# Two-layer graph network on one core: the first layer's products on 64 partitions, its loads by three chunks

## The chip, the cores and the metric

The kernel runs on one core of a Trainium2 chip. The metric is the device time of one execution, in microseconds, as the median of several runs. Engines are named as in the profile: PE is TensorE (PEld its weight loads), DVE is VectorE, ACT is ScalarE, POOL is GpSimd, SP is SyncE. SP issues nearly all plain transfers, POOL the indirect ones.

## The reference

There are N = 12500 nodes with 128 features and E = 400000 edges, sorted by their destination `dst`. With `ln` for a layer norm without weights, and a sum per destination node:

```python
h   = relu(ln(x))
e   = relu(concat(h[src], h[dst], edge_attr) @ We1 + be1)    # 320 -> 32
m   = relu(e @ We2 + be2)                                    # 32 -> 128
n   = relu(concat(h[dst], m) @ Wn1 + bn1)                    # 256 -> 64
msg = relu(n @ Wn2 + bn2)                                    # 64 -> 128
x1  = x + h + segment_sum(msg, dst)

h1  = relu(ln(x1))
H   = einsum('ni,rio->rno', h1, W)                           # 8 relations
out = x1 + relu(segment_sum((H[etype, src] + b[etype]) * weight, dst))
```

`edge_attr` has 64 values an edge; `etype` is one of 8 relations; `weight` is one number an edge.

## The kernel before, in words

**Nodes first.** A stage over all nodes (pools `n0` and `n1`) writes tables to DRAM. `tab_a` has each node's 32 values `h @ We1[:128]`, for the source side. `tab_cb` has the destination side's 64 + 32 values, split into three bf16 parts in three rows. The centring of x runs mostly on POOL. `rel_d` holds, for each chunk of edges, `dst` less the chunk's least `dst`, and other small tables hold the starts of chunks and spans.

**First layer** (pool `e0`). The edges go by chunks of 1024 (`CE` = `CT` x 128 = 8 tiles of 128): 391 chunks. Three chunks (`SC`) make a span, 131 of them, which shares one window of 128 destination nodes and one accumulator. For a chunk the class `Edges` does this:

- `gather_a` (line 358): eight indirect transfers on POOL, one for each tile of 128 edges, fetch rows of `tab_a` into `gb`. This tile has 16 buffers.
- `load_rel` (379) and `load` (373, 375): SP loads `relb` (one chunk's `rel_d`, broadcast to 126 partitions, 252 KB), `eat` (the edge attributes, turned, 256 KB) and `win` (42 nodes x 3 rows of `tab_cb`, 23.6 KB). These tiles have 4, 5 and 8 buffers.
- `ends_T` (383): DVE compares `relb` with the node numbers; `ohT`, 126 x 1024 in bf16, is a one-hot matrix of destinations.
- `first` (395, 398): PE forms `pre`, 128 partitions x 256 columns. The edges of a chunk lie as four quarters of 256 columns on four groups of 32 partitions. Two products with `w_ea` (which has We1's edge rows twice, on its diagonal) and four with `win` and `ohT`.
- `first_src` (403, 405): DVE turns the gathered rows in blocks of 32 x 32 (`agT`) and adds them to `pre`, giving `z`. `first_end` (409): ACT makes `h1` from it.
- `second` (416, 422): PE makes two tiles `pm0` and `pm1`, 128 x 512, by four products of 256 columns. Each takes 64 partitions of `h1` and a `w_e2` whose other half is zero. ACT makes `em` from them.
- `third` (428, 431, 434), `fourth` (441), `fourth_sum` and `fourth_end` (449, 450, 455): the node network, from `u` and `h2` to `pq` and `nm`. `nm` holds each message as a rounded part and the rest.
- `ends` (460) makes the one-hot matrix `oh` of the span's window, and `fifth` (465) multiplies it with `nm` into the accumulator `acc`.

The loop over chunks writes one step of several chunks at a time; step i holds `load(i + 3)`, the gather and `first` of chunk i, `second` and `third` of i - 1, `fourth` and what follows of i - 2, and `fifth` of i - 3. `in_order` makes SP, DVE, ACT and PE keep that written order; POOL has only the gathers. On SP a step's order is: loads of chunk i + 3; when i is a multiple of 3 the previous span's `xt` (631); then the stores of a span that has ended (644 `agg0_d`, 510 `x1_d`, 511 `out`); the next span's `aw` (472); and one step of `prepare`.

`prepare` makes what the second layer needs (the order of edges in `hidx_sb`, `rel_t`, `ew_sb`) by way of DRAM, one step per chunk from the first chunk on. Its tiles `raw`, `tr` and `hidx` have two buffers each.

When a span has ended, `rows_h` adds its sums to x and h, stores the rows x1 (to `x1_d`, and to `out`), and makes the second layer's table `tab_h` of 8 x 128 values for each of the window's nodes (lines 485 to 527).

**Second layer** (pool `e1`). POOL gathers a row of `tab_h` for each edge (line 950, 3128 gathers); DVE weights and adds them, PE adds them by node, and `add_out` (785 to 797) adds the sum to x1 and stores `out`. It starts when the whole of `tab_h` is written. A branch, `again`, serves inputs that this layout does not fit; it does not run here.

Of the kernel before, what the change touches and what calls it, by code (L numbers as in the profile page):

```python
# [19 lines left out]
P = 128  # L20
# [29 lines left out]
def gnn_kernel(  # L50
# [82 lines left out]
    b_e1 = const.tile([P, 1], F32, name="b_e1")  # L133
# [125 lines left out]
    with tc.tile_pool(name="n1", bufs=2) as pool:  # L259
# [103 lines left out]
    class Edges:  # L363
# [5 lines left out]
            self.pool, self.psum, self.iota, self.node = pool, psum, iota, node  # L369

        def load(self, c, row):
            self.eat = self.pool.tile([P, 512], F32, name="eat", bufs=5)
            nc.sync.dma_start(self.eat, ea[ds(c, 1), :, :].rearrange("o k e -> (o k) e"))
            self.win = self.pool.tile([WR, 96], BF16, name="win", bufs=8)
            nc.sync.dma_start(self.win, tab_cb[ds(row, WR), :])

        def load_rel(self, c):
            self.relb = self.pool.tile([WR, CE], BF16, name="relb", bufs=4)
            nc.sync.dma_start(self.relb, rel_d[c:c + 1, :].to_broadcast([WR, CE]))

        def ends_T(self):
            self.ohT = self.pool.tile([WR, CE], BF16, name="ohT", bufs=4)
# [3 lines left out]
        def ends_T_of(self, c, node):  # L386
# [14 lines left out]
        def first_src(self, gb):  # L401
            agT = self.pool.tile([P, 256], F32, name="agT", bufs=2)
            nc.vector.transpose(agT, gb.rearrange("p t f -> p (t f)"))  # L403
            self.z = self.pool.tile([P, 256], F32, name="z", bufs=2)
            nc.vector.tensor_add(self.z, self.pre, agT)  # L405

        def first_end(self):
            self.h1 = self.pool.tile([P, 256], F32, name="h1", bufs=2)
            nc.scalar.activation(self.h1, self.z, AF.Relu, bias=b_e1)  # L409

        def second(self):
            pms = [self.psum.tile([P, 512], F32, name=f"pm{h}") for h in range(2)]
            for i in range(2):
                for h in range(2):
                    rows = slice(64 * h, 64 * h + 64)
                    nc.tensor.matmul(pms[h][:, 256 * i:256 * i + 256],  # L416
                                     w_e2[rows, 2 * h + i, :], self.h1[rows, :],
                                     start=True, stop=True)
            self.em = []
            for h in range(2):  # L420
                em = self.pool.tile([P, 512], F32, name=f"em{h}", bufs=2)
                nc.scalar.activation(em, pms[h], AF.Relu, bias=b_e2)  # L422
                self.em.append(em)

        def third(self):
            u = self.psum.tile([P, 512], F32, name="u")
            for h in range(2):
                nc.tensor.matmul(u[64 * h:64 * h + 64, :], self.win[:, 0:64],
                                 self.ohT[:, 512 * h:512 * h + 512], start=True, stop=False)
# [32 lines left out]

        def fifth(self, acc, start, stop):
            for i in range(CT):
                nc.tensor.matmul(acc, self.oh[:, i, :],  # L465
                                 self.nm[:, i, :, :].rearrange("p q d -> p (q d)"),
                                 start=(start and i == 0), stop=(stop and i == CT - 1))

    def window0(pool, row, n):
# [33 lines left out]
                                       op0=OP.max, op1=OP.add)  # L503
        return x0

    def rows_h(pool, psum, row, x0, aw, banks):
# [4 lines left out]
        nc.sync.dma_start(out[ds(row, P), :], x1)  # L511
# [15 lines left out]
        nc.sync.dma_start(tab_h[ds(row, P), :], ht)  # L527


    with tc.tile_pool(name="e0", bufs=2) as pool, \  # L530
# [6 lines left out]
        chunks, spans = {}, {}  # L537
        active = []

        def node_step():  # L540
# [3 lines left out]
        def load(c):  # L544
            e = Edges(pool, psum, iota_p, nid_p)
            row = nc.values_load(cidx[0:1, c:c + 1], engines=[ENG.SP], min_val=0,
                                 max_val=3 * (N - 1),
                                 skip_runtime_bounds_check_because="a chunk's least dst is a node")
            e.load_rel(c)
            e.load(c, nc.s_assert_within(  # L550
                row, 0, 3 * (NP - WB), skip_runtime_bounds_check_because="WB < NP - N"))
            chunks[c] = e

        def prepare():
# [5 lines left out]
            for g in range(0, NTP, QT):  # L560
                m = min(QT, NTP - g)
                cols = slice(g, g + m)
                for given, table in ((dst_t, dst_d), (et, hidx_d), (ew, ew_d)):
                    raw = pool.tile([P, QT], F32, name="raw")
                    nc.sync.dma_start(raw[:, :m] if given is ew else raw[:, :m].bitcast(I32),
                                      given[:, cols])
                    yield
                    if given is dst_t:
                        nc.vector.tensor_copy(raw[:, :m], raw[:, :m].bitcast(I32))
                    elif given is et:  # L570
                        nc.vector.scalar_tensor_tensor(raw[:, :m], src_sb[:, cols], float(R),
                                                       raw[:, :m].bitcast(I32),
                                                       op0=OP.mult, op1=OP.add)
                    tr = pool.tile([P, QT], F32, name="tr")
                    nc.vector.transpose(tr[:, :m], raw[:, :m])
                    rows = table[cols, :].rearrange("(q r) (a j) -> a r q j", r=32, j=32)
                    for a in range(4):
                        nc.sync.dma_start(
                            rows[a], tr[32 * a:32 * a + 32, :m].rearrange("r (q j) -> r q j", j=32))
                    yield  # L580
            odd = pool.tile([P, NSP // QS], F32, name="odd", bufs=1)
            for i, s in enumerate(range(0, NSP, QS)):
                cols = slice(s * ST, (s + QS) * ST)
                hidx = pool.tile([P, QS * ST], F32, name="hidx")
# [235 lines left out]
    def again():  # L820
# [7 lines left out]
        with tc.tile_pool(name="g1", bufs=2) as pool, \  # L828
# [34 lines left out]
            with tc.For_i(0, NP, P) as row:  # L863
                xt = pool.tile([P, D], F32, name="xt")
                nc.sync.dma_start(xt, x[ds(row, P), :])
                x0 = plus_normed(pool, xt, *deviation(pool, xt))
                for _ in rows_h(pool, psum, row, x0, window0(pool, row, P), ("u", "u", "u")):
                    pass

        with tc.tile_pool(name="g2", bufs=2) as pool, \  # L870
# [174 lines left out]
```

## Time and profile before

| what | us |
|---|---|
| median of 5 runs | 7956.49 |
| lowest and highest | 7954.86, 7959.75 |
| the profiled execution | 7958.23 |
| its span, first to last instruction | 7956.4 |

| engine | busy us | share of the span |
|---|---|---|
| PE | 3299.8 | 41% |
| DVE | 5089.0 | 64% |
| ACT | 1627.8 | 20% |
| POOL | 5951.6 | 75% |

The share is a mean over stages that have different limits: the node stage fills some 50 us, the first layer lasts to about 4000 us and the second takes the rest. A row of the profile for a group of instructions reads: line, engine, operation, output <- inputs, count | busy us in all, mean ns of one | idle time of the engine just ahead of them, and what ended it. "issue" is time in which an engine waited for nothing that the profile shows. In the timeline a row has its start, its duration, and what it is; SPq is an issue of a transfer by SP. An f32 product of PE shows as two instructions (two passes), a bf16 or rounded one as one. A table by stage has the stretch, its length, an engine's busy us and (x) instructions, the clock that TensorE was granted, the DMA engines' busy share, and GB/s.

### The profile page before, as it was taken

Reading aid. Unit: us, or ns where it says so; the run is one execution under the profiler, and the core shown is the slowest. Engines: PE = TensorE matmul, PEld = TensorE weight load, DVE = VectorE, ACT = ScalarE, POOL = GpSimd, SP = SyncE. Lnnn points to the kernel's source line nnn. Section 1 sums busy time; section 2 is a strip of 40 time slices with the busy share of each in tenths; the row PEclk is TensorE's granted clock in tenths of the full one; section 3 lists DMA queues with packets and bytes.
Section 4 is the critical chain, followed back from the end, with each engine's and each line's share of the span. In section 5 each row is a group of like instructions: output and inputs, shape, how many; then the busy total and the mean of one; then the engine's idle time right before and its main releaser. Section 6 shows DMA issues by size and latency. Waiting matters only on the chain.

```text
span 7956.4 us, 66587 instructions
## 1 busy us (share of the span) xinstructions
PE 3299.8 (41%) x16589; PEld 1960.3 (25%) x16590; DVE 5089.0 (64%) x8155; ACT 1627.8 (20%) x3217; POOL 5951.6 (75%) x6273
## 2 busy tenths in 40 slices
PE   4877777777777777777720000000000000000000
PEld 3444444444444444444410000000000000000000
DVE  7887766666766766667655555555555555555555
ACT  3443333333333333333300000000000000000000
POOL 6777777777777777777757777777777777777776
PEclk7999899999999999999955555555555555555555
DMA  6655544333333333343322222222222222222222
GB/s 193 150 115 104 103 121 106 96 94 102 93 97 101 91 100 98 92 101 95 90 60 61 62 62 61 62 62 61 62 61 62 62 61 62 62 61 62 62 61 58
DMA packets 766351, 670.08 MB, mean 84 GB/s; under 512 B 382920, under 2 KB 587980, under 8 KB 765502
## 3 DMA queue, kind: packets, MB, share of 16 engines
q1 hardware_dynamic: 563608, 408.65, 17.8%
q0 software_dynamic: 200192, 256.65, 15.5%
q8 instruction: 135, 2.21, 0.1%
q14 instruction: 260, 2.13, 0.1%
q10 hardware_dynamic: 2156, 0.45, 0.0%
HBM read 526.07 MB, written 139.10 MB: 84 GB/s over the span
## 4 chain that ended last, share of the span: by engine, by line
POOL 55%; issue 24%; DMA 12%; DVE 6%; PE 2%; ACT 1%; SPq 1%; POOLq 0%; DVEq 0%; ACTq 0%
POOL hg L950 32%; POOL gb L358 23%; DMA gb<-tab_a,src_sb 8%; DMA hg<-tab_h,hidx_sb 2%; DVE nm L455 1%; DVE ohT L383 1%; DVE oh L460 1%; DMA xt<-in_x 0%; DVE pq L449 0%; ACT nm L450 0%; PE pq L441 0%; DMA tab_cb<-cs 0%; DVE ht L526 0%; PE acc L465 0%; DVE z L405 0%
## 5 line engine op out<-in xcount | busy, mean ns | idle before, releaser
L950 POOL DMA_INDIRECT hg<-tab_h,hidx_sb x3128 | 2954.5, 945 | 998.1 <-issue 929.6
L358 POOL DMA_INDIRECT gb<-tab_a,src_sb x3032 | 2868.9, 946 | 925.5 <-issue 828.9
L957 DVE TENSOR_TENSOR v<-hg,io_p 128x1024 f32<-128x1024 f32 x782 | 960.1, 1228 | 1689.5 <-DMA hg<-tab_h,hidx_sb 1681.6
L924 PE MATMUL acc<-hm,oh 128*128 128x256 f32 x782 | 299.6, 484 | 3621.9 <-DVE oh L921 3588.8
L924 PEld LDWEIGHTS acc<-hm,oh 128*128 128x128 f32 x782 | 195.8, 311 | 3726.8 <-issue 3692.0
L961 DVE TENSOR_REDUCE sm<-v 128x128 f32<-128x1024 f32 x782 | 958.9, 1226 | 9.0
L964 ACT CAST hm<-sm 128x256 fp32r<-128x256 f32 x391 | 145.6, 373 | 3778.2 <-DVE sm L961 3778.2
L441 PE MATMUL pq<-w_n,h 128*128 128x256 f32 x3128 | 846.0, 419 | 0.0
L403 DVE STREAM_TRANSPOSE agT<-gb 128x256 f32<-128x256 f32 x391 | 173.5, 444 | 893.7 <-DMA gb<-tab_a,src_sb 891.8
L465 PE MATMUL acc<-nm,oh 128*128 128x256 f32 x3128 | 563.5, 330 | 389.5 <-DVE a L478 280.9
L441 PEld LDWEIGHTS pq<-w_n,h 128*128 128x128 f32 x3128 | 644.3, 216 | 88.3 <-issue 0.3
L465 PEld LDWEIGHTS acc<-nm,oh 128*128 128x128 f32 x3128 | 471.7, 221 | 556.2 <-issue 356.4
L450 ACT ACTIVATE nm<-pq 128x512 fp32r<-128x512 f32 x782 | 441.8, 597 | 625.7 <-DVE pq L449 623.1
L455 DVE SCALAR_TENSOR_TENSOR nm<-pq,nm 128x512 fp32r<-128x512 f32 x782 | 503.7, 686 | 70.2 <-ACT nm L450 25.6
L449 DVE TENSOR_TENSOR pq<-pq,b_n 128x512 f32<-128x512 f32 x782 | 505.1, 691 | 1.5 <-PE pq L441 1.5
L422 ACT ACTIVATE em<-pm,b_e 128x512 f32<-128x512 f32 x782 | 491.5, 681 | 58.8 <-PE pm L416 58.1
L434 ACT ACTIVATE h<-u,b_n 128x512 f32<-128x512 f32 x391 | 268.6, 687 | 1131.7 <-PE u L431 1131.6
L416 PE MATMUL pm<-h,w_e 64*128 64x256 f32 x3128 | 493.2, 438 | 1.8 <-ACT h L409 1.8
L383 DVE TENSOR_TENSOR ohT<-relb,io_p 126x1024 bf16<-126x1024 bf16 x391 | 473.2, 1210 | 15.6 <-DMA relb<-rel_d 15.6
L460 DVE TENSOR_TENSOR oh<-io_p,rel_s 128x1024 fp32r<-128x1024 f32 x391 | 475.8, 1217 | 0.0
L431 PE MATMUL u<-em,w_msg 128*64 128x512 f32 x1564 | 415.7, 600 | 6.7 <-ACT em L422 6.5
L525 PE MATMUL u<-w_f,hT 128*128 128x512 f32 x520 | 294.3, 648 | 209.6 <-ACT h L434 206.1
(117 smaller groups left out, 3225.9 us busy)
## 6 DMA issues: line engine op xcount, KB each, us to landing
eat<-in_ea SPq DMA_DIRECT2D x391, 256.0 KB
relb<-rel_d SPq DMA_DIRECT2D x391, 252.0 KB
tab_h<-ht SPq DMA_DIRECT2D x131, 512.0 KB
hg<-tab_h,hidx_sb POOLq DMA_INDIRECT x3128
gb<-tab_a,src_sb POOLq DMA_INDIRECT x3032
aw<-agg_d SPq DMA_DIRECT2D x262, 64.0 KB
agg_d<-a SPq DMA_DIRECT2D x261, 64.0 KB
agg_d<-zeros SPq DMA_DIRECT2D x48, 256.0 KB
```

The costliest lines, as they stand in the source:

```text
L358: nc.gpsimd.indirect_dma_start(out=gb[:, t, :], out_offset=None, in_=tab_a, in_offset=bass.IndirectOffsetOnAxis(ap=idx(t), axis=0))
L383: nc.vector.tensor_tensor(self.ohT, self.relb, self.node.to_broadcast([WR, CE]), op=OP.is_equal)
L416: nc.tensor.matmul(pms[h][:, 256 * i:256 * i + 256], w_e2[rows, 2 * h + i, :], self.h1[rows, :], start=True, stop=True)
L441: nc.tensor.matmul(pq[:, 2 * i:2 * i + 2, :], self.h2[:, P * (2 * k + i):P * (2 * k + i) + P], w_n2, start=True, stop=True)
L449: nc.vector.tensor_add(pq, pq, b_n2[:, None, :].to_broadcast([P, 4, D]))
L455: nc.vector.scalar_tensor_tensor(nm[:, :, 1, :], pq, 0.0, nm[:, :, 0, :], op0=OP.max, op1=OP.subtract)
L460: nc.vector.tensor_tensor(self.oh, self.iota[:, None, :].to_broadcast([P, CT, P]), rel[:, :, None].to_broadcast([P, CT, P]), op=OP.is_equal)
L465: nc.tensor.matmul(acc, self.oh[:, i, :], self.nm[:, i, :, :].rearrange("p q d -> p (q d)"), start=(start and i == 0), stop=(stop and i == ...
L924: nc.tensor.matmul(acc[:, 0:2 * D], oh[:, q, :], hm[:, q, :, :].rearrange("p r d -> p (r d)"), start=begin and q == 0, stop=stop and q == 1)
L950: nc.gpsimd.indirect_dma_start(out=hg[:, t - c * CT, :], out_offset=None, in_=tab_hr, in_offset=bass.IndirectOffsetOnAxis(ap=hidx_sb[:, t: ...
L957: nc.vector.tensor_tensor(v, hg, w_p[:, q, t:t + CT, None].to_broadcast([P, CT, D]), op=OP.mult)
L961: nc.vector.tensor_reduce(sm[:, q, :], v.rearrange("p t d -> p d t"), AX.X, OP.add)
```

## The change

- `pre`, `z` and `h1` become 64 partitions x 512 columns. `first` has one product with `w_ea` of 512 columns and two with `win` (32 partitions and 512 columns each, the columns of `ohT` taken as two runs of 256). `z` is made by two additions of 64 x 256. `second` has two products of 512 columns, each on 32 partitions of `h1`. `w_e2` is 64 x 128 without zeros, and `b_e1` has 64 rows; their memset and four loads on ACT's queue are gone.
- The order of edges in `u` changes with it; `third` takes the same halves of `ohT`, and `fifth` the tiles of `nm` in an order that fits.
- `eat` and `relb` are loaded for three chunks by one transfer each, at the span's first chunk, into 3 and 2 buffers of that size. `win` is loaded for each chunk as before. `eat` now comes ahead of `relb`.
- `rows_h` does not store x1 to `out` in this path.
- `raw`, `tr` and `hidx` have one buffer each.

```diff
-    w_e2 = const.tile([P, 4, D], F32, name="w_e2")
+    w_e2 = const.tile([64, D], F32, name="w_e2")
...
-        nc.vector.memset(w_e2, 0.0)
...
-        for i in range(4):
-            nc.scalar.dma_start(w_e2[32 * i:32 * i + 32, i, :], we2)
+        for i in range(2):
+            nc.scalar.dma_start(w_e2[32 * i:32 * i + 32, :], we2)
             nc.scalar.dma_start(b_e1[32 * i:32 * i + 32, :], be1)
...
+        def half_T(self, h):
+            return self.ohT.rearrange("w (b a e) -> w a b e", b=2, a=2)[:, h, :, :]
+
         def first(self):
-            self.pre = self.psum.tile([P, 256], F32, name="pre")
-            for i in range(2):
-                nc.tensor.matmul(self.pre[64 * i:64 * i + 64, :], w_ea,
-                                 self.eat[:, 256 * i:256 * i + 256], start=True, stop=False)
-            for a in range(4):
-                nc.tensor.matmul(self.pre[32 * a:32 * a + 32, :], self.win[:, 64:96],
-                                 self.ohT[:, 256 * a:256 * a + 256], start=False, stop=True)
+            self.pre = self.psum.tile([64, 512], F32, name="pre")
+            nc.tensor.matmul(self.pre, w_ea, self.eat, start=True, stop=False)
+            for h in range(2):
+                nc.tensor.matmul(self.pre[32 * h:32 * h + 32, :], self.win[:, 64:96],
+                                 self.half_T(h), start=False, stop=True)
...
-            self.z = self.pool.tile([P, 256], F32, name="z", bufs=2)
-            nc.vector.tensor_add(self.z, self.pre, agT)
+            self.z = self.pool.tile([64, 512], F32, name="z", bufs=2)
+            for i in range(2):
+                cols = slice(256 * i, 256 * i + 256)
+                nc.vector.tensor_add(self.z[:, cols], self.pre[:, cols], agT[64 * i:64 * i + 64, :])
...
-            pms = [self.psum.tile([P, 512], F32, name=f"pm{h}") for h in range(2)]
-            for i in range(2):
-                for h in range(2):
-                    rows = slice(64 * h, 64 * h + 64)
-                    nc.tensor.matmul(pms[h][:, 256 * i:256 * i + 256],
-                                     w_e2[rows, 2 * h + i, :], self.h1[rows, :],
-                                     start=True, stop=True)
+            pms = []
+            for h in range(2):
+                pm = self.psum.tile([P, 512], F32, name=f"pm{h}")
+                rows = slice(32 * h, 32 * h + 32)
+                nc.tensor.matmul(pm, w_e2[rows, :], self.h1[rows, :], start=True, stop=True)
+                pms.append(pm)
...
+                at = i % 2 * 4 + i // 2 % 2 * 2 + i // 4
                 nc.tensor.matmul(acc, self.oh[:, i, :],
-                                 self.nm[:, i, :, :].rearrange("p q d -> p (q d)"),
+                                 self.nm[:, at, :, :].rearrange("p q d -> p (q d)"),
...
-        nc.sync.dma_start(out[ds(row, P), :], x1)
+        if to_out:
+            nc.sync.dma_start(out[ds(row, P), :], x1)
...
-            e.load_rel(c)
-            e.load(c, nc.s_assert_within(
+            s, k = divmod(c, SC)
+            if k == 0:
+                eat = pool.tile([P, SC, 512], F32, name="eats", bufs=3)
+                nc.sync.dma_start(eat, ea[c:c + SC, :, :].rearrange("c k e -> k c e"))
+                relb = pool.tile([WR, SC, CE], BF16, name="relb", bufs=2)
+                nc.sync.dma_start(relb, rel_d[c:c + SC, :].rearrange("(o c) e -> o c e", o=1)
+                                  .to_broadcast([WR, SC, CE]))
+                loaded[s] = eat, relb
+            eat, relb = loaded[s]
+            e.eat, e.relb = eat[:, k, :], relb[:, k, :]
+            e.load_win(nc.s_assert_within(
...
-                    raw = pool.tile([P, QT], F32, name="raw")
+                    raw = pool.tile([P, QT], F32, name="raw", bufs=1)
```

More of the change, by code (lines that the diff above doesn't have):

```diff
@@ L129, in gnn_kernel @@
     w_ea = const.tile([P, 64], F32, name="w_ea")
-    w_e2 = const.tile([P, 4, D], F32, name="w_e2")
+    w_e2 = const.tile([64, D], F32, name="w_e2")
     w_msg = const.tile([P, 64], F32, name="w_msg")
     w_n2 = const.tile([P, 2 * D], F32, name="w_n2")
-    b_e1 = const.tile([P, 1], F32, name="b_e1")
+    b_e1 = const.tile([64, 1], F32, name="b_e1")
     b_e2 = const.tile([P, 1], F32, name="b_e2")
@@ L371, in load, with load_win @@
         def load(self, c, row):
-            self.eat = self.pool.tile([P, 512], F32, name="eat", bufs=5)
+            self.eat = self.pool.tile([P, 512], F32, name="eat", bufs=2)
             nc.sync.dma_start(self.eat, ea[ds(c, 1), :, :].rearrange("o k e -> (o k) e"))
+            self.load_win(row)
+        def load_win(self, row):
             self.win = self.pool.tile([WR, 96], BF16, name="win", bufs=8)
             nc.sync.dma_start(self.win, tab_cb[ds(row, WR), :])
-        def load_rel(self, c):
-            self.relb = self.pool.tile([WR, CE], BF16, name="relb", bufs=4)
-            nc.sync.dma_start(self.relb, rel_d[c:c + 1, :].to_broadcast([WR, CE]))
         def ends_T(self):
@@ L403, in first_src @@
             nc.vector.transpose(agT, gb.rearrange("p t f -> p (t f)"))
-            self.z = self.pool.tile([P, 256], F32, name="z", bufs=2)
-            nc.vector.tensor_add(self.z, self.pre, agT)
+            self.z = self.pool.tile([64, 512], F32, name="z", bufs=2)
+            for i in range(2):
+                cols = slice(256 * i, 256 * i + 256)
+                nc.vector.tensor_add(self.z[:, cols], self.pre[:, cols], agT[64 * i:64 * i + 64, :])
         def first_end(self):
-            self.h1 = self.pool.tile([P, 256], F32, name="h1", bufs=2)
+            self.h1 = self.pool.tile([64, 512], F32, name="h1", bufs=2)
             nc.scalar.activation(self.h1, self.z, AF.Relu, bias=b_e1)
         def second(self):
-            pms = [self.psum.tile([P, 512], F32, name=f"pm{h}") for h in range(2)]
-            for i in range(2):
-                for h in range(2):
-                    rows = slice(64 * h, 64 * h + 64)
-                    nc.tensor.matmul(pms[h][:, 256 * i:256 * i + 256],
-                                     w_e2[rows, 2 * h + i, :], self.h1[rows, :],
-                                     start=True, stop=True)
+            pms = []
[4 more added lines that the diff above has]
+                pms.append(pm)
             self.em = []
@@ L428, in third @@
                 nc.tensor.matmul(u[64 * h:64 * h + 64, :], self.win[:, 0:64],
-                                 self.ohT[:, 512 * h:512 * h + 512], start=True, stop=False)
+                                 self.half_T(h), start=True, stop=False)
             for h in range(2):
@@ L504, in plus_normed, with rows_h @@
         return x0
-    def rows_h(pool, psum, row, x0, aw, banks):
+    def rows_h(pool, psum, row, x0, aw, banks, to_out=False):
         x1 = pool.tile([P, D], F32, name="x1", bufs=2)
@@ L536, in gnn_kernel @@
         nc.vector.tensor_copy(nid_p, nid)
-        chunks, spans = {}, {}
+        chunks, spans, loaded = {}, {}, {}
         active = []
@@ L573, in prepare @@
                                                        op0=OP.mult, op1=OP.add)
-                    tr = pool.tile([P, QT], F32, name="tr")
+                    tr = pool.tile([P, QT], F32, name="tr", bufs=1)
                     nc.vector.transpose(tr[:, :m], raw[:, :m])
@@ L583, in prepare @@
                 cols = slice(s * ST, (s + QS) * ST)
-                hidx = pool.tile([P, QS * ST], F32, name="hidx")
+                hidx = pool.tile([P, QS * ST], F32, name="hidx", bufs=1)
                 for table, to in ((dst_d, rel_t[:, cols]), (hidx_d, hidx), (ew_d, ew_sb[:, cols])):
@@ L866, in again @@
                 x0 = plus_normed(pool, xt, *deviation(pool, xt))
-                for _ in rows_h(pool, psum, row, x0, window0(pool, row, P), ("u", "u", "u")):
+                for _ in rows_h(pool, psum, row, x0, window0(pool, row, P), ("u", "u", "u"),
+                                to_out=True):
                     pass
```

## The prediction

> **What bounds the kernel now.** I read the page's busy shares and its chain first, then GpSimd's busy time by stage, then who waits for whom in the middle of the first layer, and last, in order of time, the stretch between the layers.
>
> ```profile
> PE 3299.8 (41%) x16589; PEld 1960.3 (25%) x16590; DVE 5089.0 (64%) x8155; ACT 1627.8 (20%) x3217; POOL 5951.6 (75%) x6273
> POOL 55%; issue 24%; DMA 12%; DVE 6%; PE 2%; ACT 1%; SPq 1%; POOLq 0%; DVEq 0%; ACTq 0%
> L950 POOL DMA_INDIRECT hg<-tab_h,hidx_sb x3128 | 2954.5, 945 | 998.1 <-issue 929.6
> L358 POOL DMA_INDIRECT gb<-tab_a,src_sb x3032 | 2868.9, 946 | 925.5 <-issue 828.9
> ```
>
> No compute engine is full; the chain is GpSimd's gathers and the "issue" between them. One gather takes 0.945 us and is followed by 0.30 us of issue: 1.25 us, eight to a chunk of 1024 edges, 10.0 us a chunk. Next, GpSimd's busy time and count of gathers, then granted clock, DMA share and GB/s; the last line lies in the second layer:
>
> ```profile
> 2000.00:2050.00 50.00, 37.79 (x40) 0.93 0.44 113
> ...
> 2004.00:2006.00 2.00, 1.70 (x2) 1.00 0.95 335
> 2016.00:2018.00 2.00, 1.39 (x3) 1.00 0.07 10
> ...
> 4150.00:4250.00 100.00, 75.62 (x81) 0.50 0.23 61
> ```
>
> Forty gathers in 50 us, whether the DMA engines are 95% or 7% busy and whatever clock TensorE has. Only the number of gathers and the time outside them make the total. From the gathers' own rows: the first starts at 53.62, the first layer's last ends at 3984.76, the second layer's run from 4030.08 to 7937.39, and the span ends at 7956.4. So 53.6 before, 3931.1 in the first layer (3128 at 1.25 would be 3910; 21 are lost at the start), 45.3 between the layers, 3907.3 in the second, 19.0 behind. The change can move only what it does to 53.6, 21 and 45.3, unless it makes the first layer's arithmetic slower than 10 us a chunk. The waits between 2000 and 3000 (100 chunks) say how far that is:
>
> ```profile
> DVE agT L403 <- DMA gb<-tab_a,src_sb: 270.0, 100, 5.0
> SPq L527 <- DVE a L477: 690.1, 34, 20.6
> ```
>
> VectorE waits 2.70 us of each chunk for the gather, 8.1 us in a span of three; SyncE is parked 20 us in each 30. That is the cover under which every first-layer edit lies. Busy time per chunk there: PE 7.56, DVE 6.96, ACT 3.68 us.
>
> **Part by part.**
>
> *First and second product.* Per chunk, from the groups between 2000 and 3000: `pre<-eat` 0.69 us (four passes of 256 columns, two column halves side by side), `pre<-ohT` 0.30, `pm<-h` 1.26 (eight passes, two row halves). After: one product of 512 columns in two passes on one column half. The row for passes one after another is `pq<-w_n,h`, 220.1 us for 800 of 256 columns, 0.275 each: 2 x 0.55 = 1.10, that is +0.41. Two `ohT` products of 512 columns: like L428, 41.8 us per 100 chunks, 0.42: +0.12. The second product is four passes of 512 in two row groups; its nearest row is `u<-em,w_msg`, four such passes in two column halves, 1.03: -0.23. PE: +0.30, 7.9 of 10 us, though eight of its matmul instructions a chunk are gone. The Trainium skill speaks against this part: in "TensorEngine Tiling (Array Packing)", "Performance Considerations", a stationary operand of at most 64 columns should be column-tiled, up to twice as fast. By that rule dropping the two halves would double the first product, +0.69 where I take +0.41, and PE would stand at 8.1. Row and rule then leave the total alone.
>
> *z and h1.* One 128x256 addition of 425 ns becomes two of 64x256. Time goes with columns, since the 128-column addition `a<-aw,acc` took 276; back-to-back additions overlap a little (two of 691 in 1.28). Bounds: +0.15 (256 columns at the 128-column price) to +0.95 (each like a 128x512 addition, 691); I take +0.40, the same columns twice: DVE 7.4 of 10. h1 goes from 501 ns to that of a 512-column activation, 681 to 687: +0.18 on ACT. All of it lies under the 2.70 us; without that cover +0.40 x 391 = 156 us. The stall stays where it is: the gather is still last.
>
> *Loads.* 782 loads of `relb` and `eat` become 262 of 756 and 768 KB; with `out` gone SyncE issues five transfers fewer a span, 0.35 us each, while parked: nothing. Bytes stay, less 131 x 64 KB. The skill's "DMA: Bandwidth & Descriptors", "Rules for kernel authors", says to coalesce many small transfers; "Anatomy of one DMA" gives a fixed 2.0 us for one (there for transfers issued from GpSimd), so 520 fewer would be an estimated 1040 us if they stood in line. Here they don't: GpSimd never waits for them. What the bundle moves is order on SyncE's queue. `xt` (L631), issued behind one chunk's 532 KB, is now behind 1548 KB; window 0 and the stores behind it likewise.
>
> ```profile
> 2008.10 0.34 SPq L631 DMA_DIRECT2D xt<-in_x  x1
> ...
> 2013.29 0.28 DVE L485 BATCH_NORM_STATS2 st<-xt 128x6 f32<-128x128 f32 x1
> ```
>
> VectorE reads it 5.2 us after its issue, without a wait. The extra 1016 KB at the 214 to 263 GB/s of 2008 to 2014 take 4.0 to 4.9 us. So VectorE waits 0 to 4.9 us a span at L485, and behind it in VectorE's order stand the next chunk's agT, z and ohT. With 3 x 0.40 for z at most 6.1 of the 8.1 us are used; I take 2, since nothing waits now. Waits for `relb` itself come later: its next group is issued some two chunks, 20 us, ahead of its first reader.
>
> *The start.* `relb` for chunk 0 lands behind 768 KB more, and group 1 is 1.5 MB instead of 0.5: the first chunks come up to 10 us later. Chunk 0's transpose starts at 134.4 now, 69.5 us behind its last gather, and the lag is down to 1.6 at chunk 47; from chunk 6 to 40 the steps average 8.8 us. With +0.4 for z and 0 to 1.6 (4.9 over three) for `xt`, 9.2 to 10.8. At the worst the lag grows from 80 by 0.8 a chunk until the preparing steps end (about chunk 90), to 147 us; `gb` has 16 buffers, 160 us of gathers, so GpSimd still never stops. From then a step is 7.3 (10 less 2.70) + 0.4 + 1.6 = 9.3 at most, and 300 chunks clear 210 us. `raw`, `tr` and `hidx` in one buffer: the next load of `raw` comes a step behind the store that already waited for `tr`, and the 38016 packets of 128 bytes to the tables took 13 ns each, 2.6 us of all 16 engines for a table, within the 15 us until `tr` is written again. Nothing. Ahead of the first gather the memset of `w_e2` (0.48 us) ended before the first `xg` landed: nothing; four ACT issues go and one `hT` moves ahead of the `sd` for which ACT stood still for 5.5 us at 28: 0 to -1.2, I take -0.5 (one quad's products). The 21 us lost early lie where VectorE's long operations run (gathers 4.8 and 4.5 us apart at 66 and 71, beside L286's 4.44); these are untouched: 0, with 3 either way.
>
> *Between the layers.* The path leaves the gather:
>
> ```profile
> 3984.66 0.33 SPq L511 DMA_DIRECT2D out<-x  x1
> 3985.63 1.33 SPq L631 DMA_DIRECT2D xt<-in_x  x2
> ...
> 3991.74 0.29 DVE L485 BATCH_NORM_STATS2 st<-xt 128x6 f32<-128x128 f32 x1 [7.57 <-DMA xt<-in_x]
> ```
>
> Without `out` the `xt` load is issued 0.65 us earlier (the spacing of L510 and L511), and no group is in front of it, since the last group went out before. Against it two z steps on VectorE's path, 2 x 0.40 = 0.80 (chunks 389 and 390), and h1 0.18. Sum +0.3; from -2 to +4.
>
> Sum: -0.5 + 0 + 0.3 = -0.2 on a span of 7956.4. The profiled execution took 7958.23, 1.8 over its span and 1.7 over the median of 7956.49. Prediction 7956.3 for the median.
>
> **The rivals.**
>
> *Slower: the bulk load in front of `xt`.* If VectorE waits at L485 so long that wait and z together pass 8.1 us in a span, the first layer becomes VectorE's, and each us beyond costs 131 us. It decides when `xt` comes 6.9 us later than now. For it: between 200 and 500 VectorE already waited 24.9 us in ten times for `xt`, and the load in the tail took 6.08 us behind the 512 KB of a `tab_h` store. Against: the bytes give at most 4.9. With 1 us too much 8087; a third of a us, 8000. Chance 0.06.
>
> *Slower: TensorE.* It stands at 7.9 us and decides at 10.0; at 10.2 a chunk, 0.2 x 391 = 78 us, it gives 8034. Chance 0.02.
>
> *Faster: the seams shrink.* The 45.3 us or the 21 would have to lose 16 in all; the profile shows 0.65 and 1.2 that can go. With a third out of the 45.3: 7941. Chance 0.03.
>
> *The change does not do what it says:* column halves lost, TensorE no lighter. Of the forecast's chance 0.7 is for this, 0.19 for halves kept some other way; it is in the sum: 7956.3 all the same.
>
> **How the numbers follow.** Forecast 0.89. In it -1.2 to 0 (start), 3 either way (early gathers), -2 to +4 (between), and 2 for the spread of five runs (7954.9 to 7959.8): added up, 7948 to 7966. A little toward the slow rivals' edge gives 7948 to 7968. A measurement of this kernel can tell 0.2%, 16 us, from no change: faster 0.03, within 0.89, slower 0.08.
>
> **What would show it.** Right: 40 gathers in every 50 us of the first layer; `agT`'s wait for `gb` down from 2.70 to about 1.6 us a chunk (2.3 if nothing waits for `xt`); `pre<-eat` near 1.1 us a chunk, z near 0.85; a new wait `st<-xt` of under 5 us a span; gap between the layers 43 to 49. Wrong: `agT`'s wait for `gb` gone, GpSimd waiting for `agT`, gathers apart by more than 1.25 us, or a first gather far from 53.

## The result, and the profile after

| | median us | lowest and highest | runs |
|---|---|---|---|
| before | 7957.05 | 7953.34, 7959.75 | 44 |
| changed | 7960.5 | 7957.2, 7963.4 | 24 |

The ratio is 1.0004, with a 95% interval from 0.9999 to 1.001: no difference that this measurement can tell from none. The profiled execution of the changed kernel took 7954.62 us, its span 7952.9.

The runs below fell on several chips: four on one where the kernel before takes 7951 us (an ordinary chip, in what follows, as is that of the table above), and eight on three others where it takes 10100 to 10211 (the slow chips). Their times are compared only with those of the kernel before on the same chip.

The page first: the engines' busy times, and the two groups of gathers.

```profile
PE 3526.3 (44%) x13461; PEld 1740.6 (22%) x13462; DVE 5297.2 (67%) x8545; ACT 1691.5 (21%) x3217; POOL 5943.6 (75%) x6273
L963 POOL DMA_INDIRECT hg<-tab_h,hidx_sb x3128 | 2951.5, 944 | 999.7 <-issue 941.1
L357 POOL DMA_INDIRECT gb<-tab_a,src_sb x3032 | 2864.2, 945 | 927.9 <-issue 798.8
```

TensorE has 3128 matmul instructions fewer and is busy for 226.5 us more; VectorE for 208 us more. POOL's gathers stand as they did: 0.945 us and 0.30 of issue. Then POOL by stage (busy us and count of instructions, granted clock, DMA share, GB/s):

```profile
2000.00:2050.00 50.00, 37.73 (x40) 1.00 0.40 111
4150.00:4250.00 100.00, 75.49 (x81) 0.50 0.23 60
```

Forty gathers in 50 us again. From the gathers' rows the parts of the span are 53.7 us ahead of the first, 3928.6 in the first layer, 46.7 between the layers, 3904.5 in the second, 19.4 behind the last (before: 53.6, 3931.1, 45.3, 3907.3, 19.0). Both layers are 2.6 to 2.8 us shorter here, the untouched one too: the period of the gathers differs by under 0.1% from one execution to another. So the shorter span of this one execution says nothing of the change.

What did change lies under that cover. VectorE's waits in the changed kernel, first from 200 to 1200 us, then from 3000 to 3900 (90 chunks); a row has the total, the times and the longest:

```profile
DVE st L487 <- DMA xt<-in_x: 156.5, 32, 10.2
DVE agT L402 <- DMA gb<-tab_a,src_sb: 5.5, 26, 0.5
```

```profile
DVE agT L402 <- DMA gb<-tab_a,src_sb: 121.4, 77, 3.9
DVE st L487 <- DMA xt<-in_x: 37.4, 22, 4.3
```

In the kernel before, from 200 to 1200:

```profile
DVE agT L403 <- DMA gb<-tab_a,src_sb: 141.3, 68, 5.9
DVE st L485 <- DMA xt<-in_x: 40.8, 18, 7.2
```

Early, VectorE now hardly waits for gathers, since it is behind them; it waits 4.9 us at each span for `xt`. The timeline of one such span:

```profile
608.01 0.40 SPq L555 DMA_DIRECT2D eats<-in_ea  x1
608.45 0.51 SPq L557 DMA_DIRECT2D relb<-rel_d  x1
...
610.25 0.37 SPq L643 DMA_DIRECT2D xt<-in_x  x1
...
618.80 0.29 DVE L487 BATCH_NORM_STATS2 st<-xt 128x6 f32<-128x128 f32 x1 [4.50 <-DMA xt<-in_x]
```

The 64 KB of `xt` go out behind 1.5 MB and are read 8.55 us after their issue; in the kernel before it was 5.2 us, without a wait, in the span shown ahead of the result (at 2008). How far VectorE falls behind is seen from each chunk's transpose `agT`: its start less the end of the chunk's last gather, worked out from the two rows.

| chunk | 0 | 6 | 30 | 50 | 90 | 120 | 150 | 200 | 300 |
|---|---|---|---|---|---|---|---|---|---|
| before, us | 69.5 | 50.3 | 21.3 | 1.6 | 2.3 | 3.6 | 1.9 | 1.5 | 2.1 |
| changed, us | 72.8 | 58.9 | 71.7 | 78.9 | 108.0 | 103.2 | 77.2 | 34.2 | 2.1 |

The lag that the kernel before worked off by chunk 47 grows until chunk 97, to 111.2 us, and is gone only by about chunk 230. POOL never stopped for it: `gb` has 16 buffers, 160 us of gathers, and at the closest POOL came to within 40 us of needing a tile that was still unread.

Two groups of TensorE and one of VectorE, from 2000 to 3000 (104 chunks; the first number behind the bar is busy us, the second the mean ns of one instruction):

```profile
L395 PE MATMUL pre<-eats,w_ea 128*64 128x512 f32 x207 | 119.2, 659 | 0.0
L417 PE MATMUL pm<-h,w_e 32*128 32x512 f32 x416 | 127.6, 692 | 0.0
L406 DVE TENSOR_TENSOR z<-pre,agT 64x256 f32<-64x256 f32 x208 | 86.6, 416 | 12.3 <-PE pre L397 0.2
```

That is 1.15, 1.23 and 0.83 us a chunk.

### The profile page after: what moved, and what is told of

It is laid out like the page before. It is cut to its first block, busy times and chain, and to the rows that moved or that the text cites. A ratio compares the mean times of both kernels' runs of the same rounds, so it can differ in the third digit from the quotient of the medians.

```text
span 7952.9 us, 59273 instructions
## 1 busy us (share of the span) xinstructions
PE 3526.3 (44%) x13461; PEld 1740.6 (22%) x13462; DVE 5297.2 (67%) x8545; ACT 1691.5 (21%) x3217; POOL 5943.6 (75%) x6273
## 5 line engine op out<-in xcount | busy, mean ns | idle before, releaser
L441 PE MATMUL pq<-w_n,h 128*128 128x256 f32 x3128 | 801.3, 402 | 0.0
L441 PEld LDWEIGHTS pq<-w_n,h 128*128 128x128 f32 x3128 | 611.0, 205 | 78.5 <-issue 0.8
L467 PE MATMUL acc<-nm,oh 128*128 128x256 f32 x3128 | 515.4, 310 | 88.5 <-DVE a L480 73.2
L467 PEld LDWEIGHTS acc<-nm,oh 128*128 128x128 f32 x3128 | 428.7, 203 | 420.8 <-issue 203.2
L395 PE MATMUL pre<-eats,w_ea 128*64 128x512 f32 x782 | 460.8, 674 | 92.3 <-DMA eats<-in_ea 91.3
L381 DVE TENSOR_TENSOR ohT<-relb,io_p 126x1024 bf16<-126x1024 bf16 x391 | 477.7, 1222 | 29.4 <-DMA relb<-rel_d 17.4
L431 PE MATMUL u<-em,w_msg 128*64 128x512 f32 x1564 | 488.7, 636 | 17.0 <-ACT em L422 16.5
L417 PE MATMUL pm<-h,w_e 32*128 32x512 f32 x1564 | 473.9, 684 | 1.9 <-ACT h L410 1.9
L528 PE MATMUL u<-w_f,hT 128*128 128x512 f32 x520 | 317.1, 694 | 206.5 <-ACT h L434 203.7
```

Of the source, the lines that this page charges most:

```text
L381: nc.vector.tensor_tensor(self.ohT, self.relb, self.node.to_broadcast([WR, CE]), op=OP.is_equal)
L441: nc.tensor.matmul(pq[:, 2 * i:2 * i + 2, :], self.h2[:, P * (2 * k + i):P * (2 * k + i) + P], w_n2, start=True, stop=True)
L467: nc.tensor.matmul(acc, self.oh[:, i, :], self.nm[:, at, :, :].rearrange("p q d -> p (q d)"), start=(start and i == 0), stop=(stop and i = ...
```

## The experiments

The theory: POOL's gathers, 1.25 us each, set the time; the layout and the loads only use up cover, the layout through VectorE and the loads through the wait for `xt`; 16 `gb` buffers are what keeps the early lag from POOL. The rivals: the lag has another cause than `xt`; the buffers are not what hides it; VectorE is the bound.

### Half the buffers, in both kernels

In `e1_after_gb8` (the changed kernel) and `e2_before_gb8` (the kernel before):

```diff
-        gb = gpool.tile([P, CT, 32], F32, name="gb", bufs=16)
+        gb = gpool.tile([P, CT, 32], F32, name="gb", bufs=8)
```

> The changed kernel with 8 buffers for gb instead of 16. Theory (GpSimd's gathers set the time and the 16 buffers hide how slow the first layer's arithmetic has become at the start): in the changed kernel's profile the gather of chunk i+8 starts up to 41 us before chunk i has been read, so GpSimd must stop for that long in all between chunks 20 and 110: 7960 + 41 = about 8000, and the gathers' own 1.25 us is seen everywhere else. Rival (the arithmetic has 8.1 us a span to spare all along, buffers don't matter): 7960.

> The kernel before with 8 buffers for gb. Theory: in its profile the gather of chunk i+8 never starts less than 15.6 us after chunk i was read, so nothing stops: 7957, within 3. Rival (half the buffers cost something by themselves, by contention or by the release of a buffer): the same loss as in the changed kernel, about 8000.

Measured on one chip, where the kernel before took 7951.22: the changed kernel 7979.89 us, ratio 1.0036 (1.0022 to 1.0051); the kernel before 7950.74, ratio 0.9999 (0.999 to 1.0009). The profiled executions took 8001.22 and 7964.42, and their first layers 3970.7 and 3933.0 us. The waits of POOL from 100 to 2000 us in `e1_after_gb8` show where:

```profile
POOL gb L357 <- DVE agT L402: 43.4, 25, 4.7
```

In the kernel before with 8 buffers that row is 0.3 us, once. Its lag is nearly that with 16 (16.7 us at chunk 35, with 16 it was 14.1), while the changed kernel's is held between 58 and 82 from chunk 6 to chunk 100: POOL has taken over the waiting. So the lag is real, and the buffers are what hides it. The size was 37 us by the profiled executions and 29 by the medians, where about 41 had been expected.

### `xt` ahead of the bulk loads

`e3_xt_first_gb8` is `e1_after_gb8` with one step moved:

```diff
-            if i + AHEAD < NC:
-                load(i + AHEAD)
             if i % SC == 0 and i:
                 spans[i // SC - 1] = Span(i // SC - 1)
+            if i + AHEAD < NC:
+                load(i + AHEAD)
```

> The changed kernel with 8 buffers for gb, and the span's xt issued ahead of the three-chunk loads instead of behind them. Theory (the lag comes from xt waiting behind 1.5 MB): VectorE's wait for xt between 200 and 1200 falls from 156 us to about 40 as before the change, the step there from 10.6 to about 9.4 us a chunk, the lag shrinks from the start, and the time is 7957 to 7965 although there are 8 buffers. Rival (the lag comes from the longer z, h1 and first product, or the DMA engines are simply busy with the bulk whatever the order): about 8000, as with 8 buffers alone.

Measured: 7953.73 us, ratio 1.0003 (0.9993 to 1.0012). VectorE's waits from 200 to 1200, first in `e1_after_gb8`, then here:

```profile
DVE st L487 <- DMA xt<-in_x: 157.8, 32, 11.2
```

```profile
DVE agT L402 <- DMA gb<-tab_a,src_sb: 93.8, 33, 7.4
...
DVE st L487 <- DMA xt<-in_x: 2.7, 1, 2.7
```

The wait for `xt` is gone, VectorE waits for gathers again, and the lag falls from 55.0 us at chunk 6 to 3.4 at chunk 50, with the new layout in place. What made the lag grow was the place of one 64 KB load in SyncE's queue.

### The layout without the coalesced loads

`e5_layout_alone` has the products, `z`, `h1` and the order of edges of the changed kernel; the loads of `eat` and `relb`, the store to `out` and the buffers of `raw`, `tr` and `hidx` are those of the kernel before. Against the changed kernel:

```diff
-            s, k = divmod(c, SC)
-            if k == 0:
...
-            e.eat, e.relb = eat[:, k, :], relb[:, k, :]
-            e.load_win(nc.s_assert_within(
+            e.relb = pool.tile([WR, CE], BF16, name="relb", bufs=4)
+            nc.sync.dma_start(e.relb, rel_d[c:c + 1, :].to_broadcast([WR, CE]))
+            e.load(c, nc.s_assert_within(
```

> The 64-partition layout alone: eat and relb loaded for one chunk at a time as before the change, x1 still stored to out, 16 buffers for gb. Theory (xt behind the bulk load makes the lag): the lag starts near 70 us as in both and falls by some 0.7 us a chunk (a step of 8.8 + 0.4 = 9.3 between chunks 6 and 40), gone by chunk 110; wait for xt between 200 and 1200 near 41 us; time 7957 to 7961. Rival (the layout makes it): the lag rises to about 100 us at chunk 90.

Measured in one run: 7953.31 us, beside 7951.22 for the kernel before. VectorE's waits from 200 to 1200:

```profile
DVE st L487 <- DMA xt<-in_x: 51.8, 25, 4.6
DVE agT L402 <- DMA gb<-tab_a,src_sb: 40.7, 31, 6.1
```

The lag falls from 53.9 us (chunk 6) to 25.5 (45) and 1.5 (80). From chunk 6 to 40 a chunk takes 9.35 us where the kernel before takes 8.81; of these 0.54 us `z` is 0.41. With `e3_xt_first_gb8` this parts the two bundles: the layout slows the catching up, the loads turn it round.

### On the slow chips: the loads alone, `z` twice, the order at the seam

Four kernels met chips where the kernel before took 10210 us and, for `e7r_z_twice` and `e6br_tail_before`, 10100; `e7_z_twice` and `e6b_tail_before` come three times under three names. `e4_loads_alone` is the kernel before with the loads by three chunks and the single buffers of `raw`, `tr` and `hidx`; it still stores to `out`. `e7_z_twice` writes each addition of `z` of the changed kernel twice:

```diff
-                nc.vector.tensor_add(self.z[:, cols], self.pre[:, cols], agT[64 * i:64 * i + 64, :])
+                for _ in range(2):
+                    nc.vector.tensor_add(self.z[:, cols], self.pre[:, cols],
+                                         agT[64 * i:64 * i + 64, :])
```

`e6_tail` (the changed kernel) and `e6b_tail_before` (the kernel before) rewrite only the order at the end of the first layer:

```diff
+            if i == L - 2:
+                for s in range((L - 1) // SC, NS):
+                    spans[s] = Span(s)
             next(prepared, None)
...
         for s in range((L - 1) // SC, NS):
-            if s not in spans:
-                spans[s] = Span(s)
-                spans[s].deviate()
+            spans[s].deviate()
...
         valued(L - 2)
+        chunks[L].first_src(gb)
+        chunks[L].first_end()
         node_step()
         ended(L - 2)
+        chunks[L].second()
...
-        chunks[L].first_src(gb)
-        chunks[L].first_end()
         node_step()
-        chunks[L].second()
```

> The three-chunk loads alone, on the layout of before (128 partitions by 256 columns), x1 still stored to out, 16 buffers for gb. Theory (xt behind the bulk load makes the lag, the layout adds 0.4 to 0.7 us a chunk): wait for xt between 200 and 1200 about 150 us as in the changed kernel, the lag neither falls nor rises much up to chunk 90 (10.6 less 0.5 = 10.1 us a chunk), 60 to 80 us there, and then falls faster than in the changed kernel; time 7951 to 7957. Rival (only both together make it): the lag falls as before the change, gone by chunk 50.

> The changed kernel with each of the two z additions done twice (the same values again), 0.85 us more of VectorE a chunk. Theory (what counts is the pace while behind, 10.6 us a chunk up to chunk 90 and 9.1 from 120 on in the changed kernel, and not the 1.35 us a chunk that VectorE still waits late in the layer): 11.4 and then 10.0 us a chunk, so the lag reaches the 150 us of 16 buffers near chunk 70, GpSimd is stopped for some 45 us in all, and about 150 us of lag are left at the end: the gap between the layers grows from 47 to almost 200 us, and the time is about 8150 (8090 to 8190). Rival (the late wait is all spare time): 0.85 is under 1.35, and the time is 7960.

> The changed kernel with another end of the first layer: xt of the last two spans is loaded two chunks earlier, and the last chunk's transpose, z, h1 and second product come before the sums of the two chunks ahead of it. Theory (only the seam of 46.7 us between the layers can still be shortened, and its path starts with 5.6 us of waiting for xt and has the last chunk's transpose 16.6 us behind its gather): the gap is 46.7 - 5 - 5 = about 36 us, the time 10 us shorter than the changed kernel's, that is 0.1% below before. Rival (the seam is bound by TensorE and ACT work that only moves): gap 44 to 47, no change.

> The kernel before with the same new end of the first layer. Theory: the gap goes from 45.3 to about 35 us and the time is 10 us, 0.13%, below before; since the change itself gives GpSimd nothing, this one beats both kernels. Rival: gap 43 to 46, same time as before.

> The changed kernel with each addition of z written twice (the same values into the same tile; nothing else). It asks how far the cover over the first layer's arithmetic reaches. Theory (gathers bound, VectorE waits 1.35 us a chunk for the gathers between 3000 and 3900 and 1.2 us a span for xt): two more additions of 0.42 us, +0.83 to +0.85 us a chunk on VectorE. While preparing goes on (to chunk 90) a step takes 10.7 + 0.85 = 11.5 us, so the lag grows from 59 us at chunk 6 by 1.5 a chunk and meets the 160 us of the 16 gb buffers near chunk 75; from then to the end of preparing the gathers stop for some 20 to 60 us in all. Behind it a step is 10 - 1.35 + 0.85 - 0.4 (half the xt wait) = 9.1 to 9.5 and the rest of the lag clears; the seam gains 2 x 0.85 = 1.7. So 7980 to 8030, and between 3000 and 3900 the agT wait for gb is down to about 0.5 us a chunk with 40 gathers in each 50 us. Rival A (VectorE is already the bound, the agT wait is no cover): every chunk pays, 391 x 0.85 = 332, 8290. Rival B (the early lag is bounded by something else than VectorE): GpSimd never waits for agT, 7960 to 7965.

> The kernel before with the order at the seam between the layers rewritten alone: the last span's xt is loaded two steps earlier, and the last chunk's agT, z and h1 are written ahead of the chunk before's second product and what follows it. Theory (the seam is a chain behind the last gather, in which the xt load's landing and the order on VectorE stand one behind the other): the gap between the layers goes from 45.3 to 35 us or so (33 to 40), nothing else moves, 7947 if the kernel before runs at 7957 (ratio 0.9985 to 0.9993). Rival (the seam is bound by the chain of products and the store of tab_h, not by xt or the order): the gap stays at 43 to 46 and the time does not move.

> The kernel of e7_z_twice once more. If it falls on a chip where the kernel before takes about 7957, the theory (gathers bound, 1.35 us a chunk of cover at 3000 to 3900) gives: lag meets the 160 us of the 16 gb buffers near chunk 75, gathers stop for 20 to 60 us in all before preparing ends, then a step of 9.1 to 9.5 clears it, agT's wait for gb between 3000 and 3900 about 0.5 us a chunk; 7980 to 8030. Rival A (VectorE is already the bound): 391 x 0.85 more, 8290. Rival B (the early lag is not VectorE's): GpSimd never waits for agT, 7960 to 7965. If it falls on a chip where the kernel before takes over 10000: near 9830 again, GpSimd waiting for agT throughout.

> The kernel of e6b_tail_before once more, against the kernel before. Theory (the 45.3 us between the layers hold the xt load's landing and VectorE's order one behind the other): the gap falls to 33 to 40 us, ratio 0.9985 to 0.9993. Rival (the chain of products and the store of tab_h bound it): gap 43 to 46, ratio 1. Where the kernel before takes over 10000, the gap is 154 to 163 and a gain of 10 us would not be told from none.

| run | us | before there | ratio (95%) | first layer us | between us |
|---|---|---|---|---|---|
| `e4_loads_alone` | 10163.03 | 10209.83 | one run | 5550.4 | 173.8 |
| `e7_z_twice` | 9847.12 | 10209.83 | one run | 5223.7 | 184.8 |
| `e6_tail` | 9824.79 | 10209.83 | 0.9627 (0.9608 to 0.9647) | 5216.9 | 168.4 |
| `e6b_tail_before` | 10197.76 | 10209.83 | 0.999 (0.9978 to 1.0002) | 5598.1 | 163.0 |
| `e7r_z_twice` | 9827.02 | 10100.51 | one run | 5206.3 | 184.6 |
| `e6br_tail_before` | 10096.16 | 10100.51 | 0.999 (0.9979 to 1.0002) | 5504.6 | 154.0 |
| `e7s_z_twice` | 9858.7 | 10210.88 | one run | 5231.4 | 189.4 |
| `e6bs_tail_before` | 10207.61 | 10210.88 | 0.9992 (0.9981 to 1.0003) | 5591.3 | 162.7 |

What binds there is seen in `e6bs_tail_before`: the page's chain and gathers, and POOL's wait from 2000 to 3000.

```profile
POOL 31%; PE 21%; issue 18%; another core or an unknown queue 18%; ACT 5%; DVE 5%; DMA 1%; SPq 0%; DVEq 0%; ACTq 0%; POOLq 0%
L358 POOL DMA_INDIRECT gb<-tab_a,src_sb x3032 | 2861.3, 944 | 2593.0 <-DVE agT L403 1695.2
L951 POOL DMA_INDIRECT hg<-tab_h,hidx_sb x3128 | 3322.5, 1062 | 1195.9 <-issue 936.0
```

```profile
POOL gb L358 <- DVE agT L403: 313.7, 43, 11.7
```

A gather of the first layer costs the same 0.944 us, but POOL stands for `agT`: the lag is at 210 to 240 us from chunk 20 on and the 16 buffers are full nearly from the start. The chain gives 18% to a queue that it cannot name, and the second layer, which the change does not touch, takes 4356 us instead of 3907, with the same gathers at 1.06 us. SyncE's issues behind the end of a span, again in `e6bs_tail_before`:

```profile
3005.97 0.35 SPq L527 DMA_DIRECT2D tab_h<-ht  x1
...
3009.57 0.70 SPq L510 DMA_DIRECT2D x_d<-x  x1
3012.41 0.71 SPq L511 DMA_DIRECT2D out<-x  x1
...
3022.32 0.00 SPq L631 DMA_DIRECT2D xt<-in_x  x1
```

From the `tab_h` store to the `xt` load are 16.4 us here. Such spans are not the rule: over all 131 the median is 6.6 us, with 17.0 the longest, and in `e6_tail` the median is 15.7; the kernel before on the ordinary chip has 5.0.

The rows of all engines say where most of the time goes. In the first layer of `e6bs_tail_before` there are 265 stretches of more than 2 us in which TensorE, VectorE and ScalarE stand idle together, 1232 us in all; in `e6_tail`, with the new layout, 171 with 1286 us. On the ordinary chip it was 5 with 31 us before the change and 18 with 67 after.

So these runs do not answer what they were sent for: how far the cover reaches where gathers bind, the loads' own share of the `xt` wait, and what the order at the seam gives where the seam is 45 us all stay open. In three runs the order at the seam gave 0.999, 0.999 and 0.9992, which is the 10 us expected, but each interval takes in 1. On one chip the gap between the layers is shorter with the new order, 163.0 against the 173.8 of `e4_loads_alone` and 168.4 against the 184.8 of `e7_z_twice`, but these kernels differ in more than the order. It was the one version that could have beaten both kernels.

They do show what happens to this change where the gathers do not bind. Kernels with the old layout have first layers of 5505 to 5598 us, those with the new one 5206 to 5231, and `e6_tail` is 3.7% faster than the kernel before. The idle stretches of all three engines do not explain that: between `e6b_tail_before` and `e6_tail`, on one chip, they do not shrink (1235 and 1286 us; with `z` twice they are 1002 to 1132). The loads have a small part in it (`e4_loads_alone`: 10163, one run, under the lowest of the 17 runs before, 10183.72). The layout and the missing store to `out` were not parted there: every run with the one has the other. Nor is VectorE the bound there: on one chip `e7_z_twice` has VectorE busy for 321.3 us more than `e6_tail` (5644.4 and 5323.1) and its first layer is 6.7 us longer. TensorE's busy time does not explain it either: on one chip it is 3765.7 us in `e6br_tail_before` and 3821.9 in `e7r_z_twice`, whose first layer is 298 us shorter. The new layout gives it 3128 matmul instructions and as many weight loads fewer. That their number is what counts there is only argued, and why the engines stand idle together on these chips was not found.

## Why the prediction was right

The forecast was 7956.3, within 7948 to 7968, and "no change"; it came out so, 7960.5, for the reason given: POOL's gathers, which nothing in the change touches, stayed 1.25 us apart. By its own steps:

**First and second product.** Taken +0.30 us a chunk on TensorE; measured between 3000 and 3900 +0.54 (734.5 less 685.7 us, by 90). The first product was near (1.10 taken, 1.15 measured). The term that failed is the second: 1.03 taken by the row `u<-em,w_msg`, two column halves, but two row groups of 32 partitions took 1.23, hardly less than the eight passes before (1.26). The nearest row was the wrong kind of halving; `pm<-h` itself, as many columns in two row groups, would have foretold it. The Trainium skill, in "TensorEngine Tiling (Array Packing)", has column tiling for a left operand of at most 64 columns ("Performance Considerations") and up to twice the speed for it ("Theoretical Speedup"). Giving it up for `pre<-eats` cost a factor of 1.67 here (0.69 to 1.15), in the rule's direction and short of its limit. TensorE stands at 8.2 of 10 us, so none of it reached the time. The case "TensorE no lighter" inside the forecast is what happened.

**`z` and `h1`.** `z` taken at 0.85, measured 0.83. (Its lower bound was worked out a little wrong: two additions at 276 ns less 425 are +0.13, not +0.15; nothing rests on it.) `h1` took 709 ns where 681 to 687 were taken.

**Loads.** "Nothing" for the transfers saved was right: 520 fewer, and POOL's rhythm is the same. For `xt` the range was 0 to 4.9 us a span and 2 was taken. It was 4.9 where VectorE is behind (156.5 us in 32 waits) and 1.2 where it is on time (37.4 us over 30 spans). The bound was right and the value chosen was too low for the first stretch, since there `xt` is read as soon as it lands; later the wait for gathers has already covered most of it. The Trainium skill, in "DMA: Bandwidth & Descriptors", "Rules for kernel authors", says to coalesce small transfers; these were of 252 and 256 KB, above the 64 KB under which it calls a transfer mostly overhead. In the changed kernel on the ordinary chip that gave nothing and made VectorE's wait for a small transfer behind them 156.5 us in place of 40.8 between 200 and 1200; on a slow chip the one run of the loads alone was 47 us shorter, against the 1040 that was worked out, as an estimate, from the page's fixed cost.

**The lag.** The worst step was taken as 10.8 us a chunk, measured 10.7 from chunk 40 to 90 and 10.5 from 6 to 40; the peak came near where it was put, at chunk 97 instead of 90. It was 111, not 147: it began from 59 at chunk 6, not 80, and grew by 0.6 a chunk, not 0.8. Behind it 9.3 was taken as the most and 9.1 measured from chunk 120 to 200 (10.0 from 90 to 120, of it 0.3 the one wait of 10.2 us that is told of last). `e1_after_gb8` shows what this step was worth: had there been 8 buffers, the change would have cost 0.36%.

**`agT`'s wait for `gb`.** 1.6 us a chunk expected from 2.70; measured 1.35 (121.4 us, 90 chunks) from 3000 on, and 0.74 between 2000 and 3000, where the lag is still being cleared. Of the fall, 0.41 is `z`, 0.42 is `xt` and 0.30 a wait of `nm` for ACT that hardly stood there before (29.4 us in place of 2.7); the rest was not followed up.

**The start.** -0.5 taken; the first gather came at 53.73, before at 53.62: nothing. The early gathers are 4.59 and 4.46 us apart, before 4.82 and 4.45.

**Between the layers.** +0.3 taken from -2 to +4; 46.68 against 45.32. The seam's timeline:

```profile
3983.27 1.30 SPq L643 DMA_DIRECT2D xt<-in_x  x2
...
3987.85 0.29 DVE L487 BATCH_NORM_STATS2 st<-xt 128x6 f32<-128x128 f32 x1 [5.63 <-DMA xt<-in_x]
...
4028.98 1.02 POOL L963 DMA_INDIRECT hg<-tab_h,hidx_sb  x1 [46.68 <-DVE io_p L927]
```

`xt` is read 5.55 us behind the last gather, 1.43 earlier than before, but not by the step that was forecast: the load is issued 0.96 us behind that gather, before 0.87, so the 0.65 us of an earlier issue did not come (the `tab_h` store ahead of it went out 0.45 us later). It was read 4.58 us after its issue instead of 6.11. The end of the chain is later all the same. But `e2_before_gb8`, whose code here is the kernel before's, had 46.99, so 1.4 us is within what the seam does by itself.

**The rivals.** The bulk load in front of `xt` had its mechanism right and decided nothing: with the lag worked off it needed 6.9 us a span, and 1.2 came. In the first 90 chunks 4.9 came, and with `z` and the preparing steps that was enough to make VectorE slower than the gathers there; the 16 buffers held it. TensorE, at 8.2, stayed below its 10. Neither seam shrank.

**What is left open** is whether the 3.45 us between the medians are anything. The interval takes in no difference at all, but the lowest of the 24 changed runs, 7957.2, lies above the median of the 44 before, so a loss of some 3 us is not ruled out.

## What to carry to other kernels

Price an edit by the stage's own limit first: here 0.5 us more of TensorE, 0.4 of VectorE and 520 fewer transfers a run all came to nothing, because one gather each 1.25 us set the pace. But cover is stock as well as rate: while a stage is catching up it has no slack, and the buffers ahead of the bound are what pays, so work out how far the lag grows and hold it against them. When loads are bundled, look at what small, soon-needed load is then queued behind the bundle, and issue that one first.

## What the runs showed of the hardware that was not expected

Behind a store of 128 x 4 bytes, `odd_d<-most`, issued once when preparing ends, other transfers come late. In the changed kernel's timeline:

```profile
1052.19 0.39 SPq L622 DMA_DIRECT2D odd_d<-most  x1
...
1067.46 0.94 POOL L357 DMA_INDIRECT gb<-tab_a,src_sb  x1 [4.15 <-DMA gb<-tab_a,src_sb]
1069.04 0.29 DVE L487 BATCH_NORM_STATS2 st<-xt 128x6 f32<-128x128 f32 x1 [10.22 <-DMA xt<-in_x]
```

From 1056 to 1062 the DMA engines moved 33 to 54 GB/s while bulk loads were queued; `xt` came 10.2 us late and POOL stood for 4.15 us, its longest stop after the first 135 us. In the kernel before the DMA engines moved 20 to 40 GB/s some 6 to 12 us behind the same store and POOL stopped for 1.26 us; in `e5_layout_alone` they moved 35 GB/s, and no gather stood longer than 0.32 us. That the store itself is the cause was not tried.

The other surprise is the slow chips: the same kernel took 27% to 28% longer there, with the same 0.944 us for a first-layer gather, 1.06 instead of 0.945 for one in the second layer, and a mean granted clock of 0.65 where the ordinary chips had 0.71.
